# A four-layer convolution stack on one core: layer 0's images prepared together and ahead of W, other DRAM layouts for the images and for the impulse response

## The chip, the cores and the metric

The kernel runs on one core of one Trainium2 chip. The metric is the device time of one execution in microseconds (us). Every time in the text is in us unless it says ns. The engines are called as in the profile: PE (TensorE matmul), PEld (weight load), DVE (VectorE), ACT (ScalarE), POOL (GpSimd) and SP (SyncE, which here only issues DMAs).

## The reference

The input x has 4 batches of 32 x 32 pixels with 16 channels, in float32. Four residual layers follow one another, each fed with a group normalisation of x (8 groups of 2 channels, statistics over all pixels).

```python
def conv_ref(inputs, M, Wp, G):                       # layers 0, 1, 2
    first = einsum('ijpq,bpqc->bijc', M2, inputs)     # M2, W2: (32,32,32,32)
    K = transpose(G, (2,3,4,0,1,5)).reshape(3, 3, 16, 32*32*16)
    shifted = conv(inputs, K, padding='SAME').reshape(b, h, w, h, w, f)
    diff = relu(inputs[:, :, :, None, None, :] - shifted)
    second = einsum('ijpq,bpqijc->bijc', W2, diff)
    return first - second

x = x + conv_ref(_gn(x), M0, Wp0, G0)                 # and so for layers 1 and 2
x = x + iir_ref(_gn(x), h0, numerators, denumerator)  # layer 3
```

So each of the layers 0 to 2 convolves the image with 1024 x 16 filters of 3 x 3 x 16, takes a ReLU of the difference and sums it over all pixels with weights W. Layer 3 divides two small polynomials in the frequency domain, transforms the quotient back to a 32 x 32 impulse response for each pair of channels, and convolves x with it.

## The kernel before, in words

**A conv layer.** The 1024 x 16 filters of a layer are cut into 128 blocks of 128 filters. One *unit* is one block and one batch: `conv_layer` (L315) issues six PE instruction lines at L351 (three stationary operands `ga`, `gb`, `gn` times two image halves), which fill one of four PSUM buffers, and then one DVE instruction of 128x1024 (L359, tile `junk`), which takes the minimum with zero, multiplies by a row of W and accumulates. A layer has 512 units. PE can be four units ahead of DVE, since PSUM has four buffers for them.

**Jobs.** The first and the last eight blocks of a layer are worked for two batches at a time: job 0 is blocks 0 to 7 with batches 0 and 1, job 1 the same blocks with batches 2 and 3. In between come jobs of eight blocks with all four batches. At a layer's end batches 0 and 1 are finished first, so that their image for the next layer is made beside the last job, and the image of batches 2 and 3 is made beside the next layer's job 0.

**W, G and M.** W arrives in pieces of two blocks, 1 MB each when spread over the 128 partitions (`load_w`, L289; six buffers). Job 0 and job 1 of a layer use the same four pieces, here called w0 to w3. G arrives in chunks of eight blocks (`load_g`, L250), as two loads `ga`, two loads `gb` and one `g9`; `prepare_g` (L268) subtracts a constant on POOL, casts on ACT and subtracts on DVE. All of them are issued on SP, except `gb` of the first chunk, which goes through ACT. `beside` (L321) puts the first term of the layer (M) and, in layer 0, the impulse response between the units.

**Images.** `make_image(a, xt)` (L144) normalises batches 2a and 2a+1 (`group_norm`, L106), splits the result into three kinds (whole, high part, low part) in the SBUF tile `y`, with the shifted rows of the edges in `e`, stores them to DRAM (`img`: L159 on SP, L163 and L164 on ACT), and after a `yield` loads 24 shifted copies into the tiles `im` (L177, 67.5 KB each, in turn on SP, ACT and POOL). It is a generator: `todo`, `step` and `drain` (L306 to L313) advance it between units.

**The start.** In layer 0 image 0 is made first. Then w0 (in two parts), w1 and w2 are issued on SP, and the generator of image 1 is started, so that its normalisation and store run between the first units. w3 is loaded by a line of its own:

```python
if len(wts) == 3 and k == 3:      # L339, in job 0 after block 3 has begun
    list(load_w())
```

**Order of DMAs.** The program sets the order of each queue, since the schedule is manual. Each DMA on SP's and ACT's hardware queues signals one of eight semaphores, in turn over both queues, and waits for the DMA that used that semaphore before it. So at most eight are under way, and a later one can wait for an earlier one that it has nothing else to do with.

**Layer 3.** `impulse_response` (L380) runs beside layer 0 and stores its result to the DRAM tile `hd` (L497, L503 on POOL), one row for each pair of channels. `load_toeplitz(k)` (L509) loads a tile `t` of 1.28 MB in eight DMAs (L516), in turn on SP and ACT, each for 16 partitions and shifted by one element. There are eight such tiles and five buffers (`TB`). Five are loaded beside layer 2, the other three at the end, when the first matmuls on `t` (L606) have freed their buffers. The tiles are used in the order 1, 7, 6, 5, 4, 3, 2, 0; the three late ones are tiles 3, 2 and 0.

Of the kernel before, what the change touches and what calls it, by code (L numbers as in the profile page):

```python
# [29 lines left out]
F32 = mybir.dt.float32  # L30
F32R = mybir.dt.float32r
AF = mybir.ActivationFunctionType
ALU = mybir.AluOpType
# [4 lines left out]
P = 128  # L38
B, C, S = 4, 16, 32
NBLK = 128  # L40
TAPS = [0, 1, 3, 4, 2, 5, 6, 7, 8]
ROW = 2 * 4 * 34
RUN = ROW - 2
# [2 lines left out]
NF = S * NK  # L46
FCH = [(f, min(P, NF - f)) for f in range(0, NF, P)]
PITCH = 40
HLEN = 8 + S * PITCH
TQ = 4  # L50
TB = 5

# [2 lines left out]
def conv_stack_kernel(ctx, tc, x, M, W, G, den, num, h0, cst, dft, one, idp, idq, out):  # L55
    nc = tc.nc
# [21 lines left out]
    xs = xp.tile([P, B, NBLK], F32, tag="x", name="x")  # L78
# [9 lines left out]
    for a in range(2):  # L88
        ys.append(const.tile([P, 3, 2, 4, 34], F32, name=f"y{a}"))
        nc.gpsimd.memset(ys[a], 0.0)  # L90
        ye.append(const.tile([P, 3, 2, 4, 34], F32, name=f"e{a}"))
        nc.gpsimd.memset(ye[a], 0.0)
        img.append(dram.tile([3, 10, C, ROW], F32, name=f"img{a}"))
    hd = dram.tile([C * C, HLEN], F32, name="hd")
    fd = dram.tile([P, B, 2, 2, S], F32, name="fd")
    td = dram.tile([NK, 2, S, 2 * P], F32, name="td")

    def group_sums(s):

        pt = pair_psum()  # L100
        for h in range(2):
            rows = slice(64 * h, 64 * h + 64)
            nc.tensor.matmul(pt[:, h, :2], lhsT=avg[rows], rhs=s[rows], start=True, stop=True)  # L103
        return pt

    def group_norm(xt):  # L106


        s = small.tile([P, 2], F32, tag="s", name="s")
        nc.vector.tensor_reduce(s, xt, AX.X, ALU.add)  # L110
        yield
        pm = group_sums(s)
        mean = small.tile([P, 2], F32, tag="mean", name="mean")
        nc.vector.tensor_copy(mean, pm[:, 0, :2])
        nc.vector.tensor_tensor(mean, mean, pm[:, 1, :2], ALU.add)
        xc = work.tile([P, 2, NBLK], F32, tag="xc", name="xc")
        nc.vector.tensor_tensor(
            xc, xt, mean.unsqueeze(2).to_broadcast([P, 2, NBLK]), ALU.subtract
        )
        sq = work.tile([P, 2, NBLK], F32, tag="sq", name="sq")  # L120
        nc.vector.tensor_tensor(sq, xc, xc, ALU.mult)
        ss = small.tile([P, 2], F32, tag="ss", name="ss")
        nc.vector.tensor_reduce(ss, sq, AX.X, ALU.add)
        yield
        yield
        pv = group_sums(ss)
        v = small.tile([P, 2], F32, tag="v", name="v")
        nc.vector.tensor_scalar(v, pv[:, 0, :2], 1e-5, None, ALU.add)
        nc.vector.tensor_tensor(v, v, pv[:, 1, :2], ALU.add)

        r = small.tile([P, 2], F32, tag="r", name="r")
        nc.scalar.activation(r, v, AF.Sqrt)
        ri = small.tile([P, 2], F32, tag="ri", name="ri")
        nc.vector.reciprocal(ri, r)
        nc.vector.tensor_tensor(ri, ri, v, ALU.mult)
        nc.vector.tensor_tensor(r, r, ri, ALU.add)
        nc.vector.tensor_scalar(r, r, 0.5, None, ALU.mult)
        rstd = small.tile([P, 2], F32, tag="rstd", name="rstd")
        nc.vector.reciprocal(rstd, r)
        return xc, rstd.unsqueeze(2).to_broadcast([P, 2, NBLK])  # L140

    ims, yc = {}, {}

    def make_image(a, xt):  # L144


        xc, rstd = yield from group_norm(xt[:, 2 * a : 2 * a + 2])
        split = lambda t: t.rearrange("p b (cc q) -> p b cc q", q=S)
        whole, hi, lo = (ys[a][:, k, :, :, 1:33] for k in range(3))
        y = work.tile([P, 2, NBLK], F32, tag=f"yc{a}", name=f"yc{a}")  # L150
        nc.vector.tensor_tensor(y, xc, rstd, ALU.mult)
        yc[a] = y
        nc.vector.tensor_copy(hi.bitcast(F32R), split(y))
        nc.scalar.copy(whole, split(y))
        nc.vector.tensor_tensor(lo, split(y), hi, ALU.subtract)  # L155
        nc.gpsimd.tensor_copy(ye[a][96:, :, :, 1:, :], ys[a][96:, :, :, :3, :])  # L156
        nc.scalar.copy(ye[a][:32, :, :, :3, :], ys[a][:32, :, :, 1:, :])
        flat = lambda t: t.rearrange("p k b cc x -> p k (b cc x)")
        nc.sync.dma_start(  # L159
            out=img[a][:, 1:9].rearrange("k p c x -> (p c) k x"), in_=flat(ys[a])  # L160
        )
        edge = lambda p: img[a][:, p].rearrange("k c x -> c k x")
        nc.scalar.dma_start(out=edge(0), in_=flat(ye[a][7 * C :]))  # L163
        nc.scalar.dma_start(out=edge(9), in_=flat(ye[a][:C]))  # L164
        yield
        ims[a] = [
            imp.tile([P, 4, 2, 4, 34], d, tag=f"im{a}{k}", name=f"im{a}{k}")
            for k, d in enumerate((F32, F32, F32R))
        ]
        taps = [(n // 4, n % 4, 0, TAPS[n]) for n in range(8)]  # L170
        taps += [(2, n, 1 + n % 2, 8) for n in range(4)]
        jobs = [(half, *tap) for tap in taps for half in range(2)]

        jobs.sort(key=lambda job: job[4] // 3 == 2 * job[0])
        for n, (half, k, slot, which, tap) in enumerate(jobs):
            at, p = 64 * half + C * slot, 4 * half + tap // 3
            (nc.sync, nc.scalar, nc.gpsimd)[n % 3].dma_start(  # L177
                out=ims[a][k][at : at + C]
                .bitcast(F32)
                .rearrange("c l b cc x -> c l (b cc x)")[:, :, :RUN],  # L180
                in_=img[a][which, p : p + 4, :, tap % 3 : tap % 3 + RUN].rearrange(
                    "l c x -> c l x"
                ),
            )
# [123 lines left out]
    def step():  # L308
        todo[:] = [t for t in todo if next(t, t) is not t]

    def drain():
        while todo:
            step()  # L313

    def conv_layer(layer, xt, finish, side=()):  # L315
# [14 lines left out]
        for job, (blks, batches) in enumerate(jobs):  # L330
            pairs = job < 2, job >= len(jobs) - 2
            for k, blk in enumerate(blks):
# [3 lines left out]
                        list(load_w())  # L336
                elif k % 2 == 0:
                    list(load_w())
                if len(wts) == 3 and k == 3:  # L339
                    list(load_w())  # L340
                if k == (3 if job == 0 else 1):
                    load_g(layer, blk // GC + 1)
                if job and k == 6:
# [34 lines left out]
        return xn  # L378

    def impulse_response():  # L380

        with tc.tile_pool(name="fs", bufs=1) as fs, tc.tile_pool(name="ft", bufs=1) as ft:

# [78 lines left out]
        with tc.tile_pool(name="fs2", bufs=1) as fs:  # L462
# [17 lines left out]
            for part in range(4):  # L480
# [13 lines left out]
                )  # L494
                yield
            nc.gpsimd.tensor_tensor(hs[:, :, :, 0], hs[:, :, :, 0], h0s, ALU.add)
            nc.gpsimd.dma_start(  # L497
                out=hd[:, :8].rearrange("(n m) r -> n m r", m=4), in_=hs[:, 0, :4, S:]
            )
            for h in range(2):  # L500
                for l in range(2):
                    n = 64 * (2 * h + l)
                    nc.gpsimd.dma_start(  # L503
                        out=hd[n : n + 64, 8:].rearrange("m (q r) -> q m r", r=PITCH),
                        in_=hs[32 * l : 32 * l + 32, h],
                    )
            yield

    def load_toeplitz(k):  # L509

        t = tp.tile([P, C, TQ * PITCH], F32, tag="t", name="t")
        hv = hd.rearrange("(j i) t -> i j t", j=C)
        ts.append(t)
        for p in range(8):
            at = 8 + k * TQ * PITCH - p
            (nc.sync, nc.scalar)[p % 2].dma_start(  # L516
                out=t[p * C : (p + 1) * C], in_=hv[:, :, at : at + TQ * PITCH]
            )
            yield

    load_g(0, 0, nc.scalar)
    images = [make_image(a, xs) for a in range(2)]
    for _ in range(4):
        next(images[0])
    prepare_g(0, 0)
    todo.append(images[0])
    drain()
    for parts in (2, 1, 1):
        list(load_w(parts))
    todo.append(images[1])  # L530
    step()
    xs = conv_layer(0, xs, make_image, impulse_response())
    xs = conv_layer(1, xs, make_image)

# [58 lines left out]
    for n, k in enumerate(order):  # L593
        if n and n + TB - 1 < len(order):
            list(load_toeplitz(order[n + TB - 1]))
        for slot in slots[k // 2]:
            for cc in range(4):
                for tile, block, q in slot:
                    at = 31 - TQ * k - q
                    if tile is None:  # L600
                        bank, cols, width = po, slice(0, P), S
                    else:
                        bank = po if tile == block else other[block]
                        cols, width = slice(32 * tile, 32 * tile + 32), 8
                        at += 8 * block
                    nc.tensor.matmul(  # L606
                        bank[cols].rearrange("n (j r) -> n j r", j=C)[:, :, 8 * cc :],
                        lhsT=y3[:, cc, at : at + width, :].rearrange("p q b -> p (q b)"),
                        rhs=ts[n][:, :, q * PITCH : q * PITCH + S - 8 * cc],
                        start=group(tile, block) not in every[:done],  # L610
                        stop=group(tile, block) not in every[done + 1 :],
                    )
                    done += 1
# [92 lines left out]
```

## Time and profile before

| | before |
|---|---|
| median of 3 runs | 3174.87 us (3174.0 to 3175.68) |
| the profiled execution | 3174.82 us |
| its span, first to last instruction | 3173.0 us |
| PE busy | 3111.1 us (98%) |
| DVE busy | 2060.4 us (65%) |
| ACT, POOL busy | 75.9 us, 235.6 us |
| mean granted TensorE clock | 0.996 |
| DMA | 322.21 MB, mean 102 GB/s |

The profile comes from one execution, whose own time lies 1.8 above its span. A line such as "DVE L359 ... [20.10 <-DMA w<-in_W_dram]" in the timeline gives the start, the duration, the engine, the source line, output and input tiles, and in brackets how long the engine sat idle before it and what ended that. The table by windows gives, for each stretch of the span, its length, then the busy time and the number of instructions of PE, PEld, DVE, ACT and POOL, the granted PE clock, the mean busy share of the 16 DMA engines, and GB/s. The share can come out above 1, because packets of two queues overlap on one DMA engine.

### The profile page before, as it was taken

The page shows a single profiled execution, that of the slowest core. Times are in us where ns is not written, and L with a number is a line of the kernel's source. Part 1 is how long each engine was busy: PE and PEld are TensorE (multiplying, and loading weights), DVE is VectorE, ACT ScalarE, POOL GpSimd, SP SyncE. Part 2 cuts the span into 40 slices and gives each one's busy share as a digit, 9 for nine tenths or more (in the row PEclk, how much of TensorE's full clock was granted, in tenths as well). Part 3 has the DMA queues.
Part 4 walks back from the last instruction along what each step waited for, and adds up shares of the span by engine and source line. Part 5 has one row for each costly group of instructions (what it writes and reads, how often), then busy time and mean ns, then how long its engine had stood idle before and what let it go on. Part 6 is the DMA issues. An engine that isn't in the chain of part 4 may idle for free.

```text
span 3173.0 us, 38930 instructions
## 1 busy us (share of the span) xinstructions
PE 3111.1 (98%) x16076; PEld 1720.0 (54%) x16076; DVE 2060.4 (65%) x3315; ACT 75.9 (2%) x98; POOL 235.6 (7%) x240
## 2 busy tenths in 40 slices
PE   4999999999999999999999999999999999999998
PEld 2544557777777554444545445455444444444454
DVE  3666666666666766666666666676666666666662
ACT  0000000000000000000000000000000000000000
POOL 1002321000000100100000000010010000000000
PEclk9999999999999999999999999999999999999999
DMA  7654345343334564443343334365544444444304
GB/s 142 137 149 97 94 106 109 89 101 92 87 88 106 99 148 121 102 97 88 87 99 94 87 87 105 75 131 138 129 107 101 98 108 108 97 95 109 90 14 54
DMA packets 86830, 322.21 MB, mean 102 GB/s; under 512 B 10555, under 2 KB 38541, under 8 KB 62205
## 3 DMA queue, kind: packets, MB, share of 16 engines
q1 hardware_dynamic: 66664, 300.50, 40.7%
q10 hardware_dynamic: 15684, 11.96, 2.3%
q0 software_dynamic: 4304, 7.27, 1.4%
q8 instruction: 126, 2.06, 0.3%
q14 instruction: 52, 0.42, 0.1%
HBM read 313.01 MB, written 6.68 MB: 101 GB/s over the span
## 4 chain that ended last, share of the span: by engine, by line
PE 96%; DMA 3%; DVE 1%; issue 0%; ACT 0%; SPq 0%; ACTq 0%; DVEq 0%
PE pt L351 94%; DMA t<-hd 1%; DMA w<-in_W_dram 1%; PE pt L210 1%; PE pt L606 1%; DMA img<-y 0%; DMA im<-img 0%; DMA g<-in_G_dram 0%; DVE junk L359 0%; PE pt L402 0%; PE pt L445 0%; PE pt L103 0%; PE pt L484 0%; DVE x L374 0%; DVE s L110 0%
## 5 line engine op out<-in xcount | busy, mean ns | idle before, releaser
L359 DVE SCALAR_TENSOR_TENSOR junk<-pt,w 128x1024 f32<-128x1024 f32 x1536 | 1880.8, 1224 | 1030.7 <-PE pt L351 973.8
L351 PE MATMUL pt<-im,ga 64*128 64x512 f32 x6144 | 1681.2, 591 | 36.7 <-DVE junk L359 19.9
L351 PE MATMUL pt<-im,gb 64*128 64x512 f32 x6144 | 1673.0, 588 | 0.0
L351 PE MATMUL pt<-im,gn 64*128 64x512 f32 x3072 | 1347.3, 806 | 0.0
L351 PEld LDWEIGHTS pt<-im,gb 64*128 64x128 f32 x6144 | 693.2, 185 | 647.6 <-issue 571.9
L351 PEld LDWEIGHTS pt<-im,ga 64*128 64x128 f32 x6144 | 681.0, 187 | 410.9 <-DVE junk L359 249.7
L351 PEld LDWEIGHTS pt<-im,gn 64*128 64x128 f32 x3072 | 358.0, 186 | 322.4 <-issue 284.9
L277 POOL TENSOR_TENSOR ga<-ga,cs 128x1024 f32<-128x1024 f32 x48 | 113.4, 2363 | 2133.0 <-DMA ga<-in_G_dram 2132.8
L359 DVE DVE_READ_ACCUMULATOR junk<-pt,w 128x1 f32 x1536 | 127.9, 83 | 0.0
L284 DVE TENSOR_TENSOR gn<-g,gn 32x1024 fp32r<-32x1024 f32 x96 | 118.0, 1229 | 9.6 <-ACT gn L281 7.6
L281 ACT CAST gn<-g 128x1024 fp32r<-128x1024 f32 x48 | 50.2, 1047 | 2322.7 <-DMA g<-in_G_dram 1894.2
L606 PE MATMUL pt<-t,y 128*32 128x512 f32 (+4 forms) x448 | 46.2, 439 | 5.4 <-DMA t<-hd 4.6
L234 POOL DMA_DIRECT2D fd<-ft x48 | 25.1, 532 | 223.5 <-DVE ft L227 213.2
L606 PEld LDWEIGHTS pt<-t,y 128*32 128x32 f32 (+1 forms) x448 | 24.9, 124 | 26.7 <-issue 18.0
L581 DVE TENSOR_TENSOR xo<-xo,pt 32x512 f32<-32x512 f32 x5 | 3.4, 682 | 39.1 <-PE pt L606 39.1
L177 POOL DMA_DIRECT2D im<-img x48 | 24.5, 518 | 27.0 <-DMA img<-y 20.5
L210 PE MATMUL pt<-mt,yt 128*64 128x512 f32 x96 | 21.9, 598 | 0.0
L156 POOL COPY e<-y 32x612 f32<-32x612 f32 x6 | 4.2, 693 | 146.3 <-DVE y L155 146.3
L210 PEld LDWEIGHTS pt<-mt,yt 128*64 128x64 f32 x96 | 6.4, 136 | 13.7 <-issue 9.7
L423 POOL TENSOR_TENSOR H<-H,d 128x256 f32<-128x256 f32 (+1 forms) x10 | 8.3, 826 | 66.6 <-DVE d L428 66.2
L103 PE MATMUL pt<-s,cs 64*128 64x2 f32 x32 | 3.3, 262 | 9.4 <-DVE s L110 9.4
L423 POOL TENSOR_TENSOR t<-s 128x256 f32<-128x256 f32 (+1 forms) x15 | 11.3, 755 | 0.0
(68 smaller groups left out, 167.2 us busy)
## 6 DMA issues: line engine op xcount, KB each, us to landing
w<-in_W_dram SPq DMA_DIRECT2D x191, 1024.0 KB
ga<-in_G_dram SPq DMA_DIRECT2D x96, 256.0 KB
g<-in_G_dram SPq DMA_DIRECT2D x48, 512.0 KB
gb<-in_G_dram SPq DMA_DIRECT2D x94, 256.0 KB
mt<-in_M_dram SPq DMA_DIRECT2D x24, 512.0 KB
t<-hd ACTq DMA_DIRECT2D x32, 160.0 KB
t<-hd SPq DMA_DIRECT2D x32, 160.0 KB
im<-img SPq DMA_DIRECT2D x48, 67.5 KB
```

What stands on the lines that cost most here:

```text
L156: nc.gpsimd.tensor_copy(ye[a][96:, :, :, 1:, :], ys[a][96:, :, :, :3, :])
L177: (nc.sync, nc.scalar, nc.gpsimd)[n % 3].dma_start(out=ims[a][k][at : at + C] .bitcast(F32) .rearrange("c l b cc x -> c l (b cc x)")[:, :, ...
L210: nc.tensor.matmul(pf[64 * h : 64 * h + 64], lhsT=yt[:, 4 * part + k].rearrange("k b c -> k (b c)"), rhs=mts[k][:, h, :], start=(k == 0), ...
L234: nc.gpsimd.dma_start(out=fv[h, cc, b], in_=ft[at : at + C, cc])
L277: nc.gpsimd.tensor_tensor(gv, gv, mid.unsqueeze(1).to_broadcast([P, GC * 8, C]), ALU.subtract)
L281: nc.scalar.copy(gn, g9)
L284: nc.vector.tensor_tensor(lo, g9[r : r + 32], lo.bitcast(F32), ALU.subtract)
L351: nc.tensor.matmul(pt[:, half, :], lhsT=w[rows, blk % GC, :], rhs=im[rows, :, b % 2, :, :S], start=n == 0, stop=n == 2,)
L359: nc.vector.scalar_tensor_tensor(junk, pt.rearrange("p h m -> p (h m)"), 0.0, wt, ALU.min, ALU.mult, accum_out=acc[b // 2][:, b % 2, blk : ...
L423: mul = lambda o, u, w: nc.gpsimd.tensor_tensor(o, u, w, ALU.mult)
L581: nc.vector.tensor_tensor(out, out, src, ALU.add)
L606: nc.tensor.matmul(bank[cols].rearrange("n (j r) -> n j r", j=C)[:, :, 8 * cc :], lhsT=y3[:, cc, at : at + width, :].rearrange("p q b -> p ...
```

## The change

1. In layer 0, `group_norm` runs once on all four batches (instructions of 128x512 in place of two sets of 128x256). `sq` moves into the tile `junk`. In layers 1 and 2 the pairs stay.
2. `make_image` is split into `store_image` and `load_image`. At the start both images are stored, then image 0 is loaded, then w0 and w1 are issued, then image 1 is loaded, then w2 and w3. The special line for w3 goes away.
3. The image in DRAM goes from [3 kinds, 10 rows, 16 channels, 272] to [10, 16, 3, 272]: what one partition stores is now one run of 3264 bytes where it was three of 1088. The loads still read runs of 1080 bytes.
4. The impulse response in DRAM is in the order of its tiles: a partition of a `t` load is one run of 10240 bytes, where it was 16 runs of 640. Its stores have runs of 640 bytes in place of 160. The order of the input channels' pairs is changed on the host to fit, in the layout of the coefficients.

```diff
-        img.append(dram.tile([3, 10, C, ROW], F32, name=f"img{a}"))
-    hd = dram.tile([C * C, HLEN], F32, name="hd")
+        img.append(dram.tile([10, C, 3, ROW], F32, name=f"img{a}"))
+    hd = dram.tile([8 + C * HLEN], F32, name="hd")
...
-        sq = work.tile([P, 2, NBLK], F32, tag="sq", name="sq")
+        sq = junkp.tile([P, S * S], F32, tag="junk", name="sq")[:, : nb * NBLK]
...
     def make_image(a, xt):
         xc, rstd = yield from group_norm(xt[:, 2 * a : 2 * a + 2])
+        store_image(a, xc, rstd)
+        yield
+        load_image(a)
...
+        flat = lambda t: t.rearrange("p k b cc x -> p (k b cc x)")
+        rows = img[a].rearrange("p c k x -> p c (k x)")
+        nc.sync.dma_start(out=rows[1:9].rearrange("p c x -> (p c) x"), in_=flat(ys[a]))
+        nc.scalar.dma_start(out=rows[0], in_=flat(ye[a][7 * C :]))
+        nc.scalar.dma_start(out=rows[9], in_=flat(ye[a][:C]))
...
-                if len(wts) == 3 and k == 3:
-                    list(load_w())
...
+            to = hd[8:].rearrange("(i q u jr) -> u q i jr", i=C, q=S, u=4)
...
-        t = tp.tile([P, C, TQ * PITCH], F32, tag="t", name="t")
+        t = tp.tile([P, TQ, C, PITCH], F32, tag="t", name="t")
...
-                out=t[p * C : (p + 1) * C], in_=hv[:, :, at : at + TQ * PITCH]
+                out=t[p * C : (p + 1) * C].rearrange("i q j r -> i (q j r)"),
+                in_=bass.AP(src.tensor, src.offset, [[HLEN, C], [1, n]]),
...
     load_g(0, 0, nc.scalar)
-    images = [make_image(a, xs) for a in range(2)]
-    for _ in range(4):
-        next(images[0])
-    prepare_g(0, 0)
-    todo.append(images[0])
-    drain()
-    for parts in (2, 1, 1):
-        list(load_w(parts))
-    todo.append(images[1])
-    step()
+    norm = group_norm(xs)
+    while True:
+        try:
+            next(norm)
+        except StopIteration as end:
+            xc, rstd = end.value
+            break
+    store_image(0, xc[:, :2], rstd[:, :2])
+    store_image(1, xc[:, 2:], rstd[:, 2:])
+    prepare_g(0, 0)
+    load_image(0)
+    list(load_w(2))
+    list(load_w())
+    load_image(1)
+    list(load_w())
+    list(load_w())
...
-                        rhs=ts[n][:, :, q * PITCH : q * PITCH + S - 8 * cc],
+                        rhs=ts[n][:, q, :, : S - 8 * cc],
```

More of the change, by code (lines that the diff above doesn't have):

```diff
@@ L48 @@
 PITCH = 40
-HLEN = 8 + S * PITCH
+HLEN = S * C * PITCH
 TQ = 4
@@ L102, in group_sums @@
             rows = slice(64 * h, 64 * h + 64)
-            nc.tensor.matmul(pt[:, h, :2], lhsT=avg[rows], rhs=s[rows], start=True, stop=True)
+            nc.tensor.matmul(pt[:, h, : s.shape[1]], lhsT=avg[rows], rhs=s[rows], start=True, stop=True)
         return pt
     def group_norm(xt):
-        s = small.tile([P, 2], F32, tag="s", name="s")
+        nb = xt.shape[1]
+        vec = lambda name: small.tile([P, B], F32, tag=name, name=name)[:, :nb]
+        s = vec("s")
         nc.vector.tensor_reduce(s, xt, AX.X, ALU.add)
@@ L112, in group_norm @@
         pm = group_sums(s)
[L113 to L116, printed above, removed]
+        mean = vec("mean")
+        nc.vector.tensor_copy(mean, pm[:, 0, :nb])
+        nc.vector.tensor_tensor(mean, mean, pm[:, 1, :nb], ALU.add)
+        xc = work.tile([P, B, NBLK], F32, tag="xc", name="xc")[:, :nb]
         nc.vector.tensor_tensor(
-            xc, xt, mean.unsqueeze(2).to_broadcast([P, 2, NBLK]), ALU.subtract
+            xc, xt, mean.unsqueeze(2).to_broadcast([P, nb, NBLK]), ALU.subtract
         )
-        sq = work.tile([P, 2, NBLK], F32, tag="sq", name="sq")
+        sq = junkp.tile([P, S * S], F32, tag="junk", name="sq")[:, : nb * NBLK]
+        sq = sq.rearrange("p (b n) -> p b n", b=nb)
         nc.vector.tensor_tensor(sq, xc, xc, ALU.mult)
-        ss = small.tile([P, 2], F32, tag="ss", name="ss")
+        ss = vec("ss")
         nc.vector.tensor_reduce(ss, sq, AX.X, ALU.add)
@@ L126, in group_norm @@
         pv = group_sums(ss)
[L127 to L131, printed above, removed]
+        v = vec("v")
+        nc.vector.tensor_scalar(v, pv[:, 0, :nb], 1e-5, None, ALU.add)
+        nc.vector.tensor_tensor(v, v, pv[:, 1, :nb], ALU.add)
+        r = vec("r")
         nc.scalar.activation(r, v, AF.Sqrt)
-        ri = small.tile([P, 2], F32, tag="ri", name="ri")
+        ri = vec("ri")
         nc.vector.reciprocal(ri, r)
@@ L137, in group_norm @@
         nc.vector.tensor_scalar(r, r, 0.5, None, ALU.mult)
-        rstd = small.tile([P, 2], F32, tag="rstd", name="rstd")
+        rstd = vec("rstd")
         nc.vector.reciprocal(rstd, r)
-        return xc, rstd.unsqueeze(2).to_broadcast([P, 2, NBLK])
+        return xc, rstd.unsqueeze(2).to_broadcast([P, nb, NBLK])
     ims, yc = {}, {}
@@ L147, in make_image, with store_image @@
         xc, rstd = yield from group_norm(xt[:, 2 * a : 2 * a + 2])
+        store_image(a, xc, rstd)
+        yield
+        load_image(a)
+    def store_image(a, xc, rstd):
         split = lambda t: t.rearrange("p b (cc q) -> p b cc q", q=S)
@@ L157, in make_image, with load_image @@
         nc.scalar.copy(ye[a][:32, :, :, :3, :], ys[a][:32, :, :, 1:, :])
[L158 to L165, printed above, removed]
+        flat = lambda t: t.rearrange("p k b cc x -> p (k b cc x)")
[3 more added lines that the diff above has]
+        nc.scalar.dma_start(out=rows[9], in_=flat(ye[a][:C]))
+    def load_image(a):
         ims[a] = [
@@ L180, in make_image @@
                 .rearrange("c l b cc x -> c l (b cc x)")[:, :, :RUN],
-                in_=img[a][which, p : p + 4, :, tap % 3 : tap % 3 + RUN].rearrange(
+                in_=img[a][p : p + 4, :, which, tap % 3 : tap % 3 + RUN].rearrange(
                     "l c x -> c l x"
@@ L496, in impulse_response @@
             nc.gpsimd.tensor_tensor(hs[:, :, :, 0], hs[:, :, :, 0], h0s, ALU.add)
-            nc.gpsimd.dma_start(
-                out=hd[:, :8].rearrange("(n m) r -> n m r", m=4), in_=hs[:, 0, :4, S:]
-            )
+            nc.gpsimd.dma_start(out=hd[:8].unsqueeze(0), in_=hs[:1, 0, 0, S:])
+            to = hd[8:].rearrange("(i q u jr) -> u q i jr", i=C, q=S, u=4)
             for h in range(2):
                 for l in range(2):
-                    n = 64 * (2 * h + l)
                     nc.gpsimd.dma_start(
-                        out=hd[n : n + 64, 8:].rearrange("m (q r) -> q m r", r=PITCH),
-                        in_=hs[32 * l : 32 * l + 32, h],
+                        out=to[2 * h + l],
+                        in_=hs[32 * l : 32 * l + 32, h].rearrange("q (i j) r -> q i (j r)", i=C),
                     )
@@ L509, in load_toeplitz @@
     def load_toeplitz(k):
-        t = tp.tile([P, C, TQ * PITCH], F32, tag="t", name="t")
-        hv = hd.rearrange("(j i) t -> i j t", j=C)
+        t = tp.tile([P, TQ, C, PITCH], F32, tag="t", name="t")
         ts.append(t)
+        n = TQ * C * PITCH
         for p in range(8):
-            at = 8 + k * TQ * PITCH - p
+            src = hd[8 + k * n - p :]
             (nc.sync, nc.scalar)[p % 2].dma_start(
-                out=t[p * C : (p + 1) * C], in_=hv[:, :, at : at + TQ * PITCH]
+                out=t[p * C : (p + 1) * C].rearrange("i q j r -> i (q j r)"),
+                in_=bass.AP(src.tensor, src.offset, [[HLEN, C], [1, n]]),
             )
@@ L681 @@
         arrays[f"G{i}"] = g[:, :, :, TAPS].transpose(3, 4, 0, 2, 1, 5).reshape(9 * C, NBLK * P)
-    d = np.asarray(inputs["L3_conv_denumerator"]).transpose(2, 3, 1, 0)
-    n = np.asarray(inputs["L3_conv_numerators"])[0].transpose(2, 3, 1, 0)
-    arrays["den"], arrays["num"] = d.reshape(64, 2 * P), n.reshape(64, 2 * P)
-    h0 = np.asarray(inputs["L3_conv_h0"]).reshape(C, C).T
+    pairs = lambda t: t.reshape(-1, 4, 4, C).transpose(0, 1, 3, 2).reshape(-1, 2 * P)
+    arrays["den"] = pairs(np.asarray(inputs["L3_conv_denumerator"]).transpose(2, 3, 1, 0))
+    arrays["num"] = pairs(np.asarray(inputs["L3_conv_numerators"])[0].transpose(2, 3, 1, 0))
+    h0 = pairs(np.asarray(inputs["L3_conv_h0"]).reshape(C, C).T)
     arrays["h0"] = h0.reshape(2, 2, 64).transpose(1, 0, 2)
```

## The prediction

> **What bounds the kernel now.** I first read the table by windows, cut where PE starts, where it last stalls in layer 0, and where layer 3 begins.
>
> ```profile
> 0.00:24.85 24.85, 1.18 (x8) 1.03 (x9) 7.15 (x19) 3.64 (x5) 10.37 (x18) 1.00 0.83 167
> 24.85:80.45 55.60, 34.98 (x168) 18.62 (x168) 19.53 (x41) 1.31 (x3) 4.74 (x9) 0.87 0.68 130
> 80.45:1040.00 959.55, 959.55 (x4903) 631.67 (x4905) 638.15 (x996) 30.23 (x41) 106.86 (x109) 1.00 0.44 103
> 1090.00:2058.00 968.00, 968.00 (x4928) 483.25 (x4926) 642.73 (x1011) 17.21 (x17) 52.06 (x42) 1.00 0.43 101
> 2106.00:3079.00 973.00, 972.93 (x4950) 487.63 (x4946) 644.76 (x1018) 16.18 (x16) 49.68 (x41) 1.00 0.45 103
> 3117.30:3173.00 55.70, 46.20 (x449) 24.73 (x448) 4.10 (x6) 0.59 (x1) 0.00 (x0) 0.96 0.65 77
> ```
>
> From 80.45 to 3079, but for the layers' seams, PE is busy all the time, and the change takes no matmul away. There, DMA, POOL and ACT work is free as long as it isn't late. What can move is 20.6 of idle PE in the second row, what lies before it, and the idle part of the last row. The chain of waits and the timeline name both.
>
> ```profile
> 39.42 15.46 DMA img<-y
> 61.64 17.40 DMA w<-in_W_dram
> 3139.21 11.02 DMA t<-hd
> 3150.26 9.56 DMA t<-hd
> ```
>
> ```profile
> 44.51 1.23 DVE L359 SCALAR_TENSOR_TENSOR junk<-pt,w 128x1024 f32<-128x1024 f32 x1 [4.10 <-DMA w<-in_W_dram]
> 53.83 1.22 DVE L359 SCALAR_TENSOR_TENSOR junk<-pt,w 128x1024 f32<-128x1024 f32 x1 [4.08 <-DMA w<-in_W_dram]
> 79.17 1.23 DVE L359 SCALAR_TENSOR_TENSOR junk<-pt,w 128x1024 f32<-128x1024 f32 x1 [20.10 <-DMA w<-in_W_dram]
> 80.45 2.15 PE L351 MATMUL pt<-im,ga 64*128 64x512 f32 x4 [17.21 <-DVE junk L359]
> 3150.48 6.74 PE L606 MATMUL pt<-t,y 128*32 128x512 f32 x96 [1.73 <-DMA t<-hd]
> 3160.06 1.42 PE L606 MATMUL pt<-t,y 128*128 128x512 f32 x3 [2.84 <-DMA t<-hd]
> ```
>
> At the start DVE waits in turn for w1 (44.51), w2 (53.83) and w3 (79.17). PE, four units ahead, stands still until 80.45. w3 is so late because SP issues it behind image 1: that store sits behind w1 and w2 on SP's queue (39.42 to 54.88), its loads take until 61.6, and only then w3 goes out. At the end PE waits 1.73 and 2.84 for the tiles `t` that are loaded late.
>
> The DMA rates come from the windows again:
>
> ```profile
> 44.00:52.00 8.00, 6.52 (x36) 3.23 (x34) 4.93 (x8) 0.00 (x0) 0.00 (x0) 1.00 0.50 120
> 64.00:73.00 9.00, 0.00 (x0) 0.00 (x0) 0.00 (x0) 0.00 (x0) 0.00 (x0) 0.64 1.05 132
> 80.50:112.00 31.50, 31.50 (x153) 17.82 (x155) 23.19 (x35) 1.04 (x1) 2.35 (x1) 0.95 0.56 125
> 3140.00:3150.00 10.00, 8.74 (x136) 3.82 (x124) 0.68 (x1) 0.00 (x0) 0.00 (x0) 1.00 1.25 128
> ```
>
> W alone moves at 120 GB/s with half of the DMA engines busy (0.50): 9.3 a piece, as 44.51 to 53.83 says too. W beside a chunk of G (64 to 73) fills all engines and still gives 132. `t` in runs of 640 bytes (3140 to 3150) gives 128 with all engines full.
>
> **Part 1, the tail (t<-hd).** The three late tiles are 24 DMAs of 160 KB, 3.9 MB. They start at 3128.19, when PE frees the first buffer, and the last lands at about 3159.8: 124 GB/s. PE needs the second of them at 3148.75 (3150.48 - 1.73) and, without that wait, the third 6.74 later, at 3155.5. So 3.9 MB in 27.3, 144 GB/s, is enough, and both waits are gone. The new loads have runs of 10240 bytes; the trace shows none so long. The nearest is W with 8192 and 4096: at 0.50 of the engines it gives 120, so 240 for all sixteen. The lower end is today's 124, which saves nothing. I take the W row, as it is nearest in run length: even two thirds of 240 suffice. What PE then does next is its own work; the sums on DVE (L581, 2.10 together) lie beside the last 8.87 of matmuls. Saved: 1.73 + 2.84 = **4.6** (bounds 0 and 4.6). The moving operand of L606 keeps its size and only its stride changes, from 640 to 160 bytes between rows of 32 elements; no row here varies that, so I bound it by -0.5 and +0.5 and take 0.
>
> A rule of the Trainium skill speaks against this term: "DMA: Bandwidth & Descriptors", section "Specifications", holds that a transfer reaches line rate from 512 bytes on. By it 640-byte runs are already good, the term would be 0, and the whole sum 3.3 in place of 7.9. The windows above differ: 640-byte runs fill the engines at 128 GB/s, where W needs half of them for 120.
>
> **Part 2, the head.** (a) DVE runs four normalisation instructions (L110, L117, L121, L123) at 128x512 in place of 128x256. The row L621 (128x512) takes 0.69 where these take 0.42: 4 x 0.27 = 1.1. Image 0's store goes out at 12.15 in place of 11.07; it landed 3.3 later (11.07 to 14.38), so its loads start at about 15.4. (b) ACT and POOL now make and store image 1 before they load image 0: on ACT a copy 0.41, a copy 0.70, two issues of 0.35 and 0.39 and the waits between, on POOL 0.69; their loads start at about 17 and 17.6 in place of 14.39 and 14.62. All told image 0 is complete some 1.7 later, and PE starts near 27. That is hidden, since units 4 to 7 wait for w1 anyway; were that cover gone it would cost 2. (c) The 24 image loads take about 8.5 of all DMA engines (10.5 from first issue to PE's start, less 2 of latency). In the built order, 11 of image 1's 24 loads (three on ACT, eight on POOL) wait for nothing that stands behind W, so they share the engines with w0 and w1: 11/24 x 8.5 = 3.9. w1 is at hand at 44.5 + 1.7 + 3.9 = 50 (46 with no sharing, 54 if they also slow W as G does). (d) The other 13 stand behind w1: on SP in its queue, on ACT because a load waits for the semaphore that w1 holds. w2 in turn waits for that ACT load, about 3 more. So w2 and w3 go out near 53, w3 8.6 sooner than 61.64, but w2 later than the 25 of before. (e) Behind them G's second chunk follows at once. As in 64 to 73, 9 us give 1.19 MB, of which about 0.5 is G and 0.65 W; the remaining 1.4 MB of w2 and w3 go at 120. With 1.3 to start and to land each, w2 is there at 68 and w3 at 77.
>
> (f) PE: units 8 to 11 are done at about 60; units 12 to 15 need DVE's first instruction on w2: 68 + 1.25 = 69.3. The clock has dropped by then, as it did before: in 80.5 to 112 the granted mean is 0.95, so 0.05 x 31.5 = 1.6 were lost after the long stall. 4 units of 1.96 and 1.6 of slow clock: 78.8. Unit 16 needs w3: 77 + 1.25 = 78.3. So PE resumes at 78.8, at full clock and with no stall left, against 80.45 + 1.6 = 82.05: saved **3.3**. Bounds: w1 at 46 and no slowing by G gives about 9; w1 at 54 and w3 at 83 gives -2.
>
> **Part 3, without effect.** Image stores of 3264-byte runs in layers 1 and 2, hd stores of 640-byte runs on POOL, and lighter `t` loads beside layer 2 all lie under PE's unbroken work; the seams wait for DVE (L374, L110), not for images. If that cover went, an image store is 3.3. `sq` in `junk` adds an ordering on DVE alone, which has a third of its time free. POOL's prepare (L277) now stands behind image 1's copy at the start and is needed only with the first unit.
>
> **Sum.** 3.3 + 4.6 = 7.9 off the profiled 3174.82 (0.05 from the median): 3166.9. A difference of 0.2%, 6.3, is about what a measurement of this kernel can tell from no change; beyond it lies under 3168.5.
>
> **The rivals.** *Rival 1: the head saves nothing.* The new wait of w2 behind image 1's loads, and W slowed by them as by G, put w3 at 81 or later, so the old stall comes back in two pieces. For it: the same bytes must pass before unit 16 as before, and W's row shows all engines taken. Against: the old order leaves the queue empty around image 1's store. Then only 4.6 stays: 3170.2 (3168.5 to 3174). *Rival 2: the head saves 7 to 9.* G's slowing of W is peculiar to that moment (other windows with G alone reach 216 at 1.02), so w2 lands near 64 and PE resumes near 74: 3162. *Rival 3, slower: the long runs fall on few DMA engines.* W shows that a load can use only half of them. A `t` load is now 16 runs; at eight engines it gives 120 GB/s and the tail stays as it is, below that PE waits longer. At four engines, 60 GB/s, the three tiles take 65 from 3128.2, the last matmuls end 33 later, and with the head's 3.3 the time is near 3200. The page named above, in its section "Why a DMA increments its semaphore by 16 and not by 1", takes the number of engines from the largest divisor up to 16 of the slowest dimension, 16 here, which is against it; the trace holds no load of this shape.
>
> **Chances.** Forecast (3164 to 3169.5) 0.50, Rival 1 0.29, Rival 2 0.16, Rival 3 0.05. Of the forecast's 0.50, 0.42 lies under 3168.5. Faster 0.42 + 0.16 = 0.58, same 0.08 + 0.29 = 0.37, slower 0.05. The range leaves out Rival 3 and the ends of the other two: 3160.5 to 3174.
>
> **What would show it.** Right: no PE wait on `t<-hd` at L606, the last `t` landing by 3150; w3's first DVE instruction at about 77, a new PE stall of 8 to 10 in front of unit 12 and none in front of unit 16. Wrong: a window of `t` loads still at about 128 GB/s, DVE waiting for w3 after 80, or a PE wait at a seam that was not there.

## The result, and the profile after

| | before | after |
|---|---|---|
| median of 6 runs, side by side | 3175.03 (3174.0 to 3176.42) | 3175.43 (3173.08 to 3177.02) |
| ratio | | 1.0001, 95% interval 0.9988 to 1.0014 |
| the profiled execution, span | 3174.82, 3173.0 | 3173.08, 3171.3 |
| start of the last layer's statistics (DVE, L110 / L112) | 3111.29 | 3112.26 |
| from there to the end of the span | 61.7 | 59.0 |

The change makes no difference that can be measured; 3166.9 was forecast. Of run 11's five executions below, the profiled one took 7353.85, with PE's matmuls about twice as long throughout; it is left out of every comparison, and no row of it is read.

The last two rows of the table split the profiled executions in a head and a tail: all of layers 0 to 2 ends 1.0 later, the tail is 2.7 shorter. Here is where the last layer's statistics begin, before and after:

```profile
3111.29 0.42 DVE L110 TENSOR_REDUCE s<-x 128x2 f32<-128x256 f32 x1
3112.26 0.42 DVE L112 TENSOR_REDUCE s<-x 128x2 f32<-128x256 f32 x1
```

The profiled execution of after happens to be the fastest of its six, and the experiments show that tails of one and the same layout differ by more than 2.7 from one execution to the next. The 1.0 of the head is no larger than its scatter either: with before's head unchanged, run 1's last layer begins at 3110.65, and with after's head unchanged, runs 2, 4, 5, 6 and 7 have 3110.84 to 3113.14 (run 7 moves only a chunk of G).

The table by windows of after, with the same columns as in the prediction (length, PE, PEld, DVE, ACT, POOL, clock, share of the DMA engines, GB/s):

```profile
24.85:80.45 55.60, 37.55 (x150) 22.63 (x152) 14.79 (x24) 0.00 (x0) 2.10 (x5) 0.91 0.69 121
3130.00:3140.00 10.00, 9.14 (x140) 4.15 (x136) 0.69 (x1) 0.00 (x0) 0.00 (x0) 1.00 1.04 148
3140.00:3150.00 10.00, 9.05 (x141) 4.17 (x132) 0.68 (x1) 0.00 (x0) 0.00 (x0) 1.00 1.04 146
```

In the first row PE has 150 matmuls in place of 168 by 80.45, and the granted clock is 0.91 in place of 0.87; the one long stall became two. In the other two, `t` moves at 146 to 148 GB/s with the DMA engines full, where the prediction took 240.

The chain of waits and the timeline of DVE in the head:

```profile
24.75 28.65 DMA w<-in_W_dram
53.42 2.42 DMA im<-img
56.52 24.59 DMA w<-in_W_dram
82.92 47.14 PE pt L357 x214
```

```profile
53.52 1.23 DVE L365 SCALAR_TENSOR_TENSOR junk<-pt,w 128x1024 f32<-128x1024 f32 x1 [6.21 <-DMA w<-in_W_dram]
71.95 1.23 DVE L365 SCALAR_TENSOR_TENSOR junk<-pt,w 128x1024 f32<-128x1024 f32 x1 [13.18 <-DMA w<-in_W_dram]
81.64 1.22 DVE L365 SCALAR_TENSOR_TENSOR junk<-pt,w 128x1024 f32<-128x1024 f32 x1 [4.44 <-DMA w<-in_W_dram]
```

The chain has the shape that the prediction gave it: w0 and w1, then an image load that w2's issue waits for, then w2 and w3. But w1 is at hand at 53.5 (forecast 50), w2 at 72.0 (68), w3 at 81.6 (77), and PE resumes at 82.92 (78.8). Before, PE resumed at 80.45 with 1.6 still to lose at the slow clock: 82.05.

PE at the end:

```profile
3133.77 15.28 PE L618 MATMUL pt<-t,y 128*32 128x512 f32 x224 [0.86 <-DVE xo L593]
3150.27 6.67 PE L618 MATMUL pt<-t,y 128*32 128x512 f32 x96 [1.22 <-DMA t<-hd]
3158.30 8.87 PE L618 MATMUL pt<-t,y 128*128 128x512 f32 x32 [1.36 <-DMA t<-hd]
```

Both waits for `t` are still there, 2.58 together where before had 4.57.

### The profile page after: what moved, and what is told of

It is laid out like the page before. It is cut to its first block, busy times and chain, and to the rows that moved or that the text cites. A ratio compares the mean times of both kernels' runs of the same rounds, so it can differ in the third digit from the quotient of the medians.

```text
span 3171.3 us, 38906 instructions
## 1 busy us (share of the span) xinstructions
PE 3113.8 (98%) x16068; PEld 1727.0 (54%) x16068; DVE 2059.5 (65%) x3302; ACT 75.6 (2%) x97; POOL 233.6 (7%) x240
## 4 chain that ended last, share of the span: by engine, by line
PE 96%; DMA 3%; DVE 1%; issue 0%; ACTq 0%; SPq 0%; ACT 0%; POOL 0%; DVEq 0%; POOLq 0%
PE pt L357 94%; DMA w<-in_W_dram 2%; DMA t<-hd 1%; PE pt L218 1%; PE pt L618 1%; DMA im<-img 0%; DVE junk L365 0%; PE pt L103 0%; PE pt L409 0%; PE pt L452 0%; DMA x<-in_x_dram 0%; PE pt L491 0%; DVE s L112 0%; DVE x L380 0%; PE pt L205 0%
## 5 line engine op out<-in xcount | busy, mean ns | idle before, releaser
L218 PEld LDWEIGHTS pt<-mt,yt 128*64 128x64 f32 x96 | 6.4, 136 | 13.7 <-issue 9.4
```

The costliest lines, as they stand in the source:

```text
L218: nc.tensor.matmul(pf[64 * h : 64 * h + 64], lhsT=yt[:, 4 * part + k].rearrange("k b c -> k (b c)"), rhs=mts[k][:, h, :], start=(k == 0), ...
```

## The experiments

Theories after the result. *Head*: image 1's early loads slow w0 and w1 by more than the 3.9 that was forecast (rival: w2's place behind image 1 alone does it, or G's chunk beside w2 and w3). *Tail*: a `t` load is limited by something other than the length of its runs: the 16 neighbouring partitions it is written to (A1, or A2 where each group of 16 has its own limit), or its source's odd alignment (rival), or nothing but scatter between executions. Ratios are to the kernel before, run beside it on the same chip. A kernel that ran once has no ratio, and only its rows are read.

**1 and 2: one half of the change each.** The first is before with only the new layout of `hd` and `t`; the second is after with the old one.

```diff
 # e1, against before
-    hd = dram.tile([C * C, HLEN], F32, name="hd")
+    hd = dram.tile([8 + C * HLEN], F32, name="hd")
...
-                        rhs=ts[n][:, :, q * PITCH : q * PITCH + S - 8 * cc],
+                        rhs=ts[n][:, q, :, : S - 8 * cc],
 # e2, against after: the same lines the other way round
```

> The kernel before with part 4 alone (impulse response in its tiles' order, loads of t in runs of 10240 bytes). If only the tail's part brings something, and the head of the changed kernel gives it back: PE's two waits for t go from 4.6 to about 2.6 as in the changed kernel's profile, PE resumes near 80.5 in layer 0, the time is 1 to 3 below before. If the new t layout also costs somewhere else (its stores beside layer 0, its loads beside layer 2): no gain or a loss although the waits are smaller.

> The changed kernel with the old layout of the impulse response (parts 1 to 3 alone). If the head is what takes the tail's gain back: w1 near 53.5, w2 near 72, w3 near 81.6, PE resumes near 83 and the waits for t are 4.6 again, so the time is 1 to 3 above before. If the head is neutral: within 1 of before.

Tail alone: 3173.35, ratio 0.9997 (0.9988 to 1.0006). Head alone: 3175.28, ratio 1.0002 (0.9993 to 1.001). Neither half is worth anything that can be measured. PE's timeline of the tail alone, at the two places where before has its waits:

```profile
3150.76 6.67 PE L605 MATMUL pt<-t,y 128*32 128x512 f32 x96 [1.94 <-DMA t<-hd]
3158.49 8.87 PE L605 MATMUL pt<-t,y 128*128 128x512 f32 x32 [1.06 <-DMA t<-hd]
```

With 640-byte runs (head alone) the first of these waits is missing and the second is 1.68. So the waits for `t` differ between executions by as much as between the layouts. The head alone has w1 at 53.16, w2 at 71.78 and w3 at 81.12, as after has: the head's late pieces are its own and not the tail's. In the tail alone w3 comes at 77.39, 1.8 sooner than in before with the same head: so much does one head differ between executions.

**3: W ahead of image 1.**

```diff
-    load_image(1)
     list(load_w())
     list(load_w())
+    load_image(1)
```

> The changed kernel, with image 1 loaded after w3 and not between w1 and w2. Theory A (the wait of w2 behind image 1's loads and the chunk of G beside w2 and w3 make them late): w2 follows w1 after 9.3, near 63, w3 near 72, G comes behind image 1; PE then waits for image 1 until about 77, so 5 to 6 less than the changed kernel. Theory B (the bytes that must pass before unit 16 set the time, whatever their order): PE resumes at 82 to 84 as in the changed kernel, only with image 1 as the last to arrive, and the time does not move.

Measured 3167.92, ratio 0.9981 (0.9972 to 0.999). DVE's timeline, and PE's line where it resumes for good:

```profile
53.80 1.23 DVE L365 SCALAR_TENSOR_TENSOR junk<-pt,w 128x1024 f32<-128x1024 f32 x1 [5.17 <-DMA w<-in_W_dram]
63.78 1.23 DVE L365 SCALAR_TENSOR_TENSOR junk<-pt,w 128x1024 f32<-128x1024 f32 x1 [4.73 <-DMA w<-in_W_dram]
```

```profile
76.35 1.22 PE L357 MATMUL pt<-im,ga 64*128 64x512 f32 x4 [3.16 <-DVE junk L365]
```

w2 comes 8.2 sooner than in after and w3 8 sooner; PE resumes 6.6 sooner. But w1 is as late as in after (53.80): on ACT and POOL image 1's loads still run beside w0 and w1. At the last layer 4.9 of the 6.6 are left (3107.34 in place of 3112.26): the granted clock is 0.88 from 76.3 to 90, where after has 1.00 from 81.1 to 90, and 0.12 of 13.7 is 1.6. The run moves two things, though: G's second chunk, which follows on SP, now goes out at 75.5 behind image 1 in place of 57.2, so it does not say how much of the gain is G's and how much image 1's.

**4: `t` written to spread partitions.** Each of the eight loads of a tile goes to every eighth partition in place of 16 neighbours.

```diff
-                out=t[p * C : (p + 1) * C].rearrange("i q j r -> i (q j r)"),
+                out=t.rearrange("(i p) q j r -> p i (q j r)", p=8)[p],
```

> The changed kernel, with each load of t written to every eighth partition in place of 16 neighbouring ones; same source, same runs of 10240 bytes. The partitions of t then stand in another order than those of y3, so layer 3's sum is another one. Theory A (16 neighbouring partitions take data no faster than about 139 GB/s): the loads run at 200 or more and PE's waits for t go. Theory B (the source side sets the rate: the shifted starts or the rows' distance): window 3130 to 3140 stays near 148 GB/s with the engines full, and the waits stay.

One execution, 3171.37. By windows:

```profile
3130.00:3140.00 10.00, 9.14 (x140) 4.03 (x134) 0.69 (x1) 0.00 (x0) 0.00 (x0) 1.00 1.03 229
3140.00:3150.00 10.00, 10.00 (x156) 4.57 (x151) 0.68 (x1) 0.00 (x0) 0.00 (x0) 1.00 0.79 168
```

and PE at the end:

```profile
3156.59 8.90 PE L618 MATMUL pt<-t,y 128*128 128x512 f32 x32 [0.80 <-DVE xo L593]
```

The same bytes in the same runs move at 229 GB/s, and PE no longer waits for `t`. What is late next is the sum on DVE, 0.80.

**5 and 6: the loads on SP and on ACT 64 partitions apart; all sources aligned.** In the second, all eight loads of a tile start at one multiple of 512 bytes.

```diff
 # e5
-        for p in range(8):
+        for p in (0, 4, 1, 5, 2, 6, 3, 7):
...
-            (nc.sync, nc.scalar)[p % 2].dma_start(
+            (nc.sync, nc.scalar)[p // 4].dma_start(
 # e6
-    hd = dram.tile([8 + C * HLEN], F32, name="hd")
+    hd = dram.tile([128 + C * HLEN], F32, name="hd")
...
-            src = hd[8 + k * n - p :]
+            src = hd[128 + k * n :]
```

> The changed kernel, with SP loading the first four groups of 16 partitions of t and ACT the last four, so that the two loads in flight lie 64 partitions apart and not next to each other. Theory A1 (the limit belongs to a block of 32 or more neighbouring partitions, which two loads share): window 3130 to 3140 rises from 148 to 200 GB/s or more and PE's waits for t go. Theory A2 (each group of 16 partitions has a limit near 70 GB/s of its own): the rate stays near 148.

> The changed kernel, with all eight loads of a t tile reading from the same start, a multiple of 512 bytes, and not from starts shifted by 4 bytes each (layer 3's sum is then another one). If the shifted starts cost rate on the source side: 200 GB/s or more in 3130 to 3140 and no waits for t. If only the 16 neighbouring partitions count: 148 GB/s and waits as in the changed kernel.

One execution each, 3172.44 and 3172.41. Windows from 3130 to 3140, first of the loads 64 apart, then of the aligned ones:

```profile
3130.00:3140.00 10.00, 9.14 (x136) 4.02 (x132) 0.69 (x1) 0.00 (x0) 0.00 (x0) 1.00 0.99 158
```

```profile
3130.00:3140.00 10.00, 9.14 (x136) 4.03 (x132) 0.69 (x1) 0.00 (x0) 0.00 (x0) 1.00 1.03 142
```

Alignment is not it: 142, and PE waits 1.61 and 1.20 for `t`. The 158 is near the 148 of A2 and far from the 200 of A1; whether the 10 above 148 are a small help, run 10 tells.

**7: G's second chunk behind w4.**

```diff
-                if k == (3 if job == 0 else 1):
+                if k == (5 if layer + job == 0 else 3 if job == 0 else 1):
```

> The changed kernel, with G's second chunk issued behind w4 and not in front of it. If G beside w2 and w3 is what slows them: w2 near 67 and w3 near 76.5 in place of 72 and 81.6, PE resumes near 78 with a stall in front of unit 12 that is 4 to 5 shorter. If W's own bytes set it: 72 and 81 as before.

One execution, 3176.94: w2 at 71.74, w3 at 80.72, nothing changed. It does not decide on G: behind w4 it was still issued at 57.96 to 60.5, so it still ran beside w2. What G and the rest of image 1 each take from w2 stays open. Together they are seen: in after, from 56.0 to 71.9, 121 GB/s make 1.92 MB, and w2 is only 1.05 of them. On w3, run 3 gives a hint: without G it comes 9.9 behind w2, in after 9.7, so G costs w3 nothing there.

**8 and 9: the same as 3, with all of image 1's loads on SP, behind W.**

```diff
-    def load_image(a):
+    def load_image(a, queues=(nc.sync, nc.scalar, nc.gpsimd)):
...
-            (nc.sync, nc.scalar, nc.gpsimd)[n % 3].dma_start(
+            queues[n % len(queues)].dma_start(
...
-    load_image(1)
     list(load_w())
     list(load_w())
+    load_image(1, (nc.sync,))
```

> The kernel with image 1 behind w3 (run e3), with all 24 loads of image 1 on SP's queue, so that none can run beside w0 to w3. If the 11 early loads cost w0 and w1 their own bytes only (3.9): w1 near 50. If they hold the DMA engines for longer: w1 near 46.5, w2 near 56, w3 near 65. Image 1 is then the last to come, near 76, and PE resumes near 77 as in run e3, since the same bytes have to pass.

> All of image 1's loads on SP behind W, timed in rounds. If the single look was right, PE resumes at about 72.3 and the end comes 7 to 8 sooner than before: a ratio of 0.9976, and the tail keeps its waits of about 1.6 and 1.1 for t. If only the order of w2 and image 1 counts and not the early loads, the time equals that of image 1 behind W on three queues, 0.9981, and w1 is at hand at 53.8 in place of 47.4.

Run 8, one execution, gave 3165.08; run 9, the same kernel in nine executions, 3167.87, ratio 0.9976 (0.9967 to 0.9986). DVE's timeline of run 8 (w1, w2), and PE's line where it resumes:

```profile
47.44 1.22 DVE L365 SCALAR_TENSOR_TENSOR junk<-pt,w 128x1024 f32<-128x1024 f32 x1 [4.80 <-DMA w<-in_W_dram]
56.67 1.23 DVE L365 SCALAR_TENSOR_TENSOR junk<-pt,w 128x1024 f32<-128x1024 f32 x1 [3.99 <-DMA w<-in_W_dram]
```

```profile
72.34 2.17 PE L357 MATMUL pt<-im,ga 64*128 64x512 f32 x4 [6.26 <-DMA im<-img]
```

With none of image 1 beside them, w1 is 6.4 sooner than in run 3 (53.80 to 47.44). That is the cost of the early loads, measured by itself. It is larger than the scatter: w1's first unit begins at 52.71 to 53.81 in the seven executions that load image 1 early (after and runs 2 to 7), at 46.91 to 47.44 in the four that don't (runs 8, 9, 10 and 12).

What the loads take from W can be read from the bytes. Windows from 27 to 36, first of run 3, then of run 9:

```profile
27.00:36.00 9.00, 3.75 (x6) 1.44 (x6) 0.00 (x0) 0.00 (x0) 1.56 (x4) 1.00 0.93 125
27.00:36.00 9.00, 7.54 (x15) 3.65 (x17) 1.23 (x2) 0.00 (x0) 0.00 (x0) 1.00 0.59 131
```

The early loads make the DMA engines busier (0.93 in place of 0.59), but no more bytes pass. Over the whole way to w1 it is the same: 28.95 at 128 GB/s in run 3 (24.75 to 53.70), 22.65 at 128 GB/s in run 8 (24.75 to 47.40). The difference is 0.81 MB, about twelve image loads, and 6.3.

W's pieces now come 9.2 apart, and what is late last is image 1. The last layer's statistics begin at 3103.93 and 3104.08 in the two profiled executions, 8.3 and 8.2 sooner than in after. PE resumes 10.6 sooner; the rest goes to the clock, which is granted at 0.87 from 72.3 to 90 (0.13 of 17.7 is 2.3).

**10: runs 5 and 9 together.**

> The same, and the two t loads in flight lie 64 partitions apart. If the head and the tail add up, the waits for t fall from 2.6 to about 1 and the time lies 1 to 2 under that of the kernel beside it: a ratio of about 0.997. If the waits only change places, the two ratios are the same.

3168.31, ratio 0.9977 (0.9968 to 0.9987), the same as beside it without the edit. The window of the `t` loads:

```profile
3130.00:3140.00 10.00, 10.00 (x156) 4.59 (x148) 0.68 (x1) 0.00 (x0) 0.00 (x0) 1.00 1.00 131
```

131 where the same edit gave 158 in run 5: the 158 lies within the scatter, and which loads go side by side on the two queues doesn't matter in any way that these runs could tell.

**11 and 12: the head of run 9, with spread loads and with the old layout.** The edits are those of run 4 and run 2.

> Head as in the kernel with image 1 on SP behind W (PE resumes at about 72.3); each t load is written to every 8th partition, so layer 3's sum differs. If the 16 neighbouring partitions limit the t loads, the windows after 3120 show over 200 GB/s again, PE waits only 0.80 before the last 32 matmuls, for the sum, and that in every execution: the tail (from the last layer's statistics to the end) is 57.8, 1 to 4 shorter than in the looks at other t loads (58.1 to 62.9), and the ratio about 0.997. If the 229 GB/s of the one look was scatter, windows show 130 to 160 and the ratio is that of the same head with neighbouring partitions, 0.9976.

> The same head with the impulse response in its old layout, runs of 640 bytes, one step of the change undone. If the new layout saves the 2.7 of the two profiled executions, the ratio is 0.9985. If the layout is worth nothing and the 2.7 is what the t loads differ by from one execution to the next, the ratio is again 0.9976 and the tail lies between 59 and 62.

Old layout: 3167.17, ratio 0.9976 (0.9966 to 0.9986), against 0.9976 for the new layout in run 9. PE at the end:

```profile
3142.89 8.36 PE L619 MATMUL pt<-t,y 128*32 128x512 f32 x96 [3.05 <-DMA t<-hd]
3152.45 8.87 PE L619 MATMUL pt<-t,y 128*128 128x512 f32 x32 [1.19 <-DMA t<-hd]
```

So the new layout is worth nothing that these intervals, about 3 wide to either side, can tell, with either head. Spread loads: ratio 0.9964 (0.9951 to 0.9978), from four executions at 3162.48 to 3164.54. All four lie below all nine executions of run 9 (3165.04 to 3169.61), though the two intervals overlap. They also lie below all nine of run 12 (3165.39 to 3169.98), which was run beside run 11 on the same chip with the same head and the old layout: 3.6 between the medians. That is the gain of run 4's spread loads in the time; their rate in run 11 isn't known.

The tails of all profiled executions, from the start of the last layer's statistics to the end of the span, worked out as 3173.0 - 3111.29 = 61.7 for before:

| `t` loads | tails | PE's waits for `t`, sum |
|---|---|---|
| 640-byte runs (before, runs 2 and 12) | 61.7, 59.3, 63.0 | 4.57, 1.68, 4.24 |
| 10240-byte runs (after, runs 1, 3, 7, 8, 9) | 59.0, 60.8, 57.8, 62.1, 59.4, 61.7 | 0.64 to 3.00; in run 9 1.81 and 2.22 more put down to DVE |
| the same, loads 64 partitions apart (runs 5 and 10) | 58.1, 62.9 | 0.20, 2.67 |
| the same, all sources aligned (run 6) | 59.8 | 2.81 |
| the same, spread over every eighth (run 4) | 57.8 | none |

Runs 8 and 9 are one and the same kernel: 59.4 and 61.7. Their windows from 3130 to 3140 have 148 and 133 GB/s. The tail without waits for `t` (run 4) is 57.8, and those with neighbouring partitions lie 0 to 5 above that: 1.5 to 5.2 with the old layout, 0 to 4.3 with the new one as built. The order of the means (61.3 for the old layout, 60.1 for the new one as built) is that of a small gain, but the spread within each row is larger.

## Why the prediction was wrong

**The order and the frame were right.** PE starts at 27.01 (near 27), w2 is issued at 55.86, behind an image load that waits for w1's semaphore, a stall of 10.30 stands in front of unit 12 (8 to 10), and layers 1 and 2 and the seams keep their times: the last seam is 0.97 later, as the first one is (0.95). One of its own signs for wrong came in: DVE waits for w3 after 80. Step (b) had image 0 complete when PE starts; it is not. PE waits for its loads twice more, 4.20 until 34.96 and 0.46 until 37.46. That stays hidden, as (b) said of its own delay: PE ends units 0 to 7 at 53.9, and w1 is at hand at 53.5.

**Part 2 (c), the price of sharing, is the head's failed step.** It priced image 1's 11 early loads by their share of 8.5 us of all DMA engines, 3.9. Run 8 against run 3 measures 6.4 for the early loads, and w1 came at 53.5, near the upper end given (54). That price let them pass at the rate of image 0's loads (24 loads are 1.66 MB, in 8.5 us 195 GB/s). Beside W they don't: with and without them 128 GB/s pass in all, so they cost W the time that their bytes take at that rate. Eleven loads are 0.76 MB, and 0.76 MB at 128 GB/s make 5.9. The prediction had the rows for it: W alone at 120 GB/s, W beside G at 132. What holds the total there while the engines are 0.6 busy is not shown. About 1 more of (c) is its base: without early loads it had w1 at 46, and run 8 has 47.4. The steps behind it, (d) and (e), were sound: from w1 to w2's issue 2.4 (3 forecast), from there to w2 16.1 (15) and to w3 25.8 (24). So the 3.5 of (c) and 1.8 of (e), less 0.6 of (d), make w3 4.6 late. Step (f) needs w3 by 77.6 to keep 78.8; with w3 at 81.64, PE resumes at 82.92, 0.9 after the 82.05 of before. That is Rival 1's head, and the change as built spends the gap that it closes on loads that run beside W: image 1's and, from w2 on, G's chunk. Run 8 shows that the gap could be had: there, PE resumes 10.6 sooner than in after.

**Part 1, the rate of `t`, is the tail's failed step.** It put the new loads at W's 240 GB/s because W's runs are nearest in length. From 3130 to 3140 they move at 148 in after and 133 to 150 in the other executions with this layout as built, against 122 to 156 for 640-byte runs (before, runs 2 and 12): just about the 144 that the prediction found to be needed, so the waits come and go. The trace of before had the warning. The prediction read only the 128 of one window, while the window before it already had 156 GB/s with the old runs:

```profile
3130.00:3140.00 10.00, 9.14 (x147) 4.18 (x140) 0.69 (x1) 0.00 (x0) 0.00 (x0) 1.00 1.24 156
```

The row that decides is run 4's: written to spread partitions, the very same runs reach 229. That the choice of partitions holds the rate down is shown, by run 4's rate and missing waits and by run 11's times; why 16 neighbouring partitions are slower is not. And 4.6 could never be saved whole: without waits for `t` PE still waits 0.80 for DVE's sum, which the prediction laid beside the last matmuls. The end of the term was 3.8.

The rule of the Trainium skill that was weighed against this step ("DMA: Bandwidth & Descriptors", section "Specifications") did better than the W row: if a transfer is at line rate from 512 bytes on, longer runs bring nothing, so it made the term 0. On the length of the runs, runs 9 and 12 agree (0.9976 twice, each to about 0.001). That section does not cover the 229 GB/s of run 4, where only the destination differs.

**Rival 1** had the head right (saves nothing) and the tail wrong with the forecast; a case in which both terms fail together was in no rival. **Rival 2**'s head (7 to 9) needs another order: in run 8, with W ahead of all of image 1 (and so of G's second chunk), the last layer begins 7.4 sooner than before. **Rival 3** did not occur: the loads fill all engines (share 1.04).

**The best version** keeps the change's head and layouts and issues image 1 on SP behind W: 0.9976 of before, about 7 sooner. Spreading `t` would bring about 4 more by run 11's four executions. There the loads were spread without regard to which channel belongs in which partition; an order that keeps the channels in place (a load would step back by one element from shift to shift) was not tried.

## What to carry to other kernels

A transfer that is moved ahead to fill a gap is paid for by what shares the engines with it at its new place: price its bytes at the total rate that the trace shows for such a mix, not at the rate that they have alone, and put what the next work needs first into the queue ahead of it. Before a rate is taken from a row with runs of the same length, compare the destinations too. One profiled execution can flatter a term by as much as the term: compare the same part in several executions, or with only that part changed, before a wait of 2 or 3 us is counted as saved.

## What the runs showed of the hardware

- Loads of 16 partitions x 10240 bytes, each into 16 neighbouring partitions: 131 to 158 GB/s from 3130 to 3140 in nine executions, with all DMA engines busy (share 0.92 to 1.05). The same load into every eighth partition: 229 (one execution), and 3.6 off the time in four others.
- Such loads differ in rate from one execution to the next: 148 and 133 GB/s in the same window of the same kernel, and its tail by 2.3.
- Image loads with 1080-byte runs beside W delayed it by 6.4. The total rate was 128 GB/s with them (share 0.72) and without them (share 0.63).
